# A graph attention kernel: the carried row taken from column 0 of the one-hots, superchunks of up to 112 nodes, and a longer memset between gathers

## The chip, the cores and the metric

The kernel runs on one core of one Trainium2 chip. The metric is the device time of one execution in microseconds. Times of "before" are a median of three runs; durations of single instructions come from one execution that the hardware profiler recorded.

## The reference

A graph of N = 6250 nodes with D = 256 features and E = 200000 edges, sorted by destination. Each edge has 32 attributes. After a layer norm and a relu of x, two graph attention layers follow: the first has 4 heads of 64 features, the second one head of 256. Each node also has an edge to itself.

```python
def _gat(x, src, dst, ea, Wg, a_s, a_d, Wge, a_e, b, n, h, f):
    hx = (x @ Wg).reshape(n, h, f)
    he = (ea @ Wge).reshape(-1, h, f)
    al = jax.nn.leaky_relu(jnp.einsum('nhf,hf->nh', hx, a_s)[src] + jnp.einsum('nhf,hf->nh', hx, a_d)[dst] + jnp.einsum('ehf,hf->eh', he, a_e), 0.2)
    m = jax.ops.segment_max(al, dst, num_segments=n)
    al = jnp.exp(al - m[dst])
    al = al / jax.ops.segment_sum(al, dst, num_segments=n)[dst]
    out = jax.ops.segment_sum(hx[src] * al[:, :, None], dst, num_segments=n)
    return out.reshape(n, h * f) + b
...
te = jax.nn.relu(edge_attr @ We0 + be0) * jnp.exp(x @ Wo0 + bo0)[src][:, None]
s2, d2, ea2 = _add_self_loops(src, dst, te, n)
x = jax.nn.relu(_gat(x, s2, d2, ea2, Wg0, as0, ad0, Wge0, ae0, bg0, n, HEADS, PH) + x)
```

The heavy part is that a row of the table of node features is fetched for every edge, scaled by the edge's weight, and summed over the edges of each destination.

## The kernel before

Edges are cut into chunks of P = 128, one edge in each partition, and C = 24 chunks make a superchunk, a "step". Each layer has 66 steps (the last two have 14 and 13 chunks), 132 in all. Since edges are sorted, the edges of a step belong to a run of some hundred consecutive nodes; `base` is the first of them, and `loc` says which of the run each edge belongs to.

In a step k, POOL fetches the source rows: `gather` (line 918) issues an indirect DMA per chunk (line 928) into the tile G, 24 of them, and behind each a memset of a small tile `gap` (line 932), which nothing reads. G has three buffers, so the gather of step k + 3 may start when the sums of step k have been made, and POOL runs ahead of the other engines. VectorE (DVE) adds up the logits of the edges (`logits`, line 1115 onward), finds maxima by segment with scans, and multiplies G by the edges' weights (`scale`, line 1223). `onehots` (line 1051) compares `loc` with a row of the numbers 0 to 127, `k_iota`, which stands in PSUM: S has for each edge a 1 in the column of its node. `sums` (line 1227) multiplies S by G on TensorE (PE), 24 matmuls, which the profile records as 48: the tile u in PSUM holds in row j the sum of node `base` + j. ScalarE (ACT) copies u to the tile U in SBUF (`evict`, line 1236); U has three buffers. `finish`, `rows1`, `rows2` and `rows3` divide by the sum of weights, add the self loop and the bias, make the node's row of the next layer's table T1 (layer 0) or of the output (layer 1), and store it.

A node whose edges begin in one step and end in the next needs the partial sum of the first step. `carry` (line 1241) selects that row of U, the row of the step's last node, by a matmul with the column `lsel` (line 1245, one-hot of the last node) into the PSUM tile `fin`, and ACT copies it into the tile `carry` (line 1247). `carried` (line 1197, on DVE) scales it and adds it to the first edge's row of the next step's G before that step's sums.

The order of the work is written out by hand in `edges` (main loop, lines 644 to 707): for step k and its successor nx, `gather(nx)`, the logits of k, edge features of nx on PE and ACT (`rphase1`, `rphase2`), the maxima and scale of k, `carried`, `sums`, then `edge_rows` and `onehots` of nx, `finish` of the step before, `evict`, `carry`, `rows1`. The last steps of a layer go through `tight` (line 727) and `last` (line 789), in which the sums are made in pieces and `carry` stands in other places. `nodes` (line 989) loads the rows of T and x of a step's nodes into the tile tw with SP's queue, 128 rows each, from a row that `base_i` gives; tw has five buffers.

Every engine works off its own queue in order. A wait of an instruction holds all that stands behind it on its engine.

Of the kernel before, what the change touches and what calls it, by code (L numbers as in the profile page):

```python
# [36 lines left out]
ED = 32  # L37
PH = 64
BIG = 1e38
PAD_DST = 1 << 20  # L40
END_DST = 1 << 22
EPS = 1e-5
# [36 lines left out]
class Kernel:  # L79
# [31 lines left out]
    def consts(self, wp):  # L111
# [33 lines left out]
                       allow_small_or_imprecise_dtypes=True)  # L145

        self.kps = k = self.ps_k.tile([P, 512], F32, name="kps")
        V.tensor_copy(k[:, 0:P], self.iota_f)
        m32 = wp.tile([P, 1], F32, name="m32", bufs=1)
        self.quad = cp.tile([P, 4], F32, name="quad")  # L150
        nc.gpsimd.memset(self.quad, 0.0)
# [2 lines left out]
            nc.gpsimd.memset(m32[r, :], -32.0 * i)  # L154
            nc.gpsimd.memset(self.quad[r, i:i + 1], 1.0)
        V.tensor_add(k[:, P:P + 1], self.iota_p, m32)
        self.k_iota, self.k_part, self.k_w = k[:, 0:P], k[:, P:P + 1], k[:, 2 * P:2 * P + 4 * C + 4]
        self.wea = []
        for L in self.L:
            wea = cp.tile([P, PH], F32, name=f"wea{L.l}")  # L160
# [236 lines left out]
    def fixed_rows(self):  # L397
        nc, cp = self.nc, self.cp
        self.crow = cp.tile([1, D + self.L[0].H], F32, name="crow")
        self.cl = [cp.tile([36, P + 1], F32, name=f"cl{i}") for i in range(2)]  # L400
        for t in self.cl:
            nc.gpsimd.memset(t, -BIG)

        self.cnt = cp.tile([P, self.NS, 2], F32, name="cnt")
        self.mt = cp.tile([P, 4 * C + 4], F32, name="mt")
        self.gap = cp.tile([P, 128], F32, name="gap")
        self.fb = [cp.tile([P, 37 * C], F32, name=f"fb{i}") for i in range(2)]
        for t in [self.mt] + self.fb:
            nc.gpsimd.memset(t, 0.0)


        self.aq = [cp.tile([P, 4, 32], BF, name=f"aq{i}") for i in range(2)]
        for t in self.aq:
            nc.gpsimd.memset(t, 0.0)
        self.trow1 = []
        L1 = self.L[1]
        for i in range(2):
            self.trow1.append(cp.tile([P, 2 * L1.TW], F32, name=f"t1row{i}"))
            nc.gpsimd.memset(self.trow1[i][:, L1.TW + D:], 0.0)
# [10 lines left out]
    def indices(self, wp):  # L430
# [26 lines left out]
        V.tensor_sub(qd, base.unsqueeze(1).to_broadcast([P, 4, NS]), qbase)  # L457
        yield
        self.qsel = cp.tile([P, NS, 4], F32, name="qsel")
        V.tensor_scalar(self.qsel.rearrange("p s k -> p k s"), qd, self.iota_p, None, op0=OP.add)  # L460
        yield

        bcf = wp.tile([NS, 4], F32, name="bcf", bufs=1)
# [29 lines left out]
        yield  # L493
        self.base_i = cp.tile([1, 2, NS], I32, name="base_i")
        V.tensor_copy(self.base_i[:, 0, :], base[0:1, :])
        V.tensor_scalar(self.base_i[:, 1, :], base[0:1, :], float(N - P), None, op0=OP.min)
        yield
        ll = wp.tile([P, NS], F32, name="ll", bufs=1)
        V.tensor_sub(ll, last, base)
        self.lsel = cp.tile([P, NS], F32, name="lsel")  # L500
        V.tensor_scalar(self.lsel, ll, self.iota_p, None, op0=OP.is_equal)
        yield
        self.slink = cp.tile([1, NS], F32, name="slink")
        V.tensor_tensor(self.slink, sc0[0:1, 0, :], sc0[0:1, 2, :], op=OP.is_equal)
# [2 lines left out]

        chk = wp.tile([1, 9, NS + 1], F32, name="chk", bufs=1)
        V.memset(chk, 0.0)
        V.tensor_scalar(chk[:, 0, :NS], ll[0:1, :], float(P - 1), None, op0=OP.is_gt)  # L510
        V.tensor_sub(qd[0:1], qlast[0:1], qbase[0:1])
        V.tensor_scalar(chk[:, 5:9, :NS], qd[0:1], 31.0, None, op0=OP.is_gt)
        nb = wp.tile([1, NS + 1], F32, name="nb", bufs=1)
# [1 line left out]
        yield  # L515
        V.memset(nb[:, NS:], float(N))
        V.tensor_sub(nb[:, :NS], nb[:, 1:], nb[:, :NS])
        V.tensor_scalar(chk[:, 1, :NS], nb[:, :NS], float(P), None, op0=OP.is_gt)
        V.tensor_scalar(chk[:, 2, :NS], nb[:, :NS], 0.0, None, op0=OP.is_lt)
        yield  # L520
        V.tensor_tensor(chk[:, 3, :NS], sc0[0:1, 0, :], sc0[0:1, 2, :], op=OP.is_lt)
        if self.direct:
            V.tensor_scalar(chk[:, 4, :self.direct], base[0:1, :self.direct], float(N - P), None, op0=OP.is_gt)
        V.memset(self.bad[:, 0:1], 0.0)
        V.tensor_reduce(self.bad[0:1, 0:1], chk.rearrange("p a b -> p (a b)"), axis=AX.X, op=OP.add)
        yield
# [84 lines left out]
    def edges(self, ctx):  # L611
# [11 lines left out]
        steps = self.steps  # L623
        self.state = {0: None, 1: None}
        self.early = 0
        self.nodes(steps[0])
        self.gather(steps[0], self.CX)
        if self.NS % 2:
# [15 lines left out]
        for k, st in enumerate(steps):  # L644
            nx = steps[k + 1] if k + 1 < len(steps) else None
            for q in steps[k + 1:k + 3]:
                if q["L"] is st["L"] and "tw" not in q:
                    self.nodes(q)
            self.load_lb(k + 2)
            left = self.groups[self.ahead][0] - 2 - k if self.ahead < len(self.groups) else 99  # L650
            if self.rest is None and left <= 2:
                gi = self.index_load(self.ahead, self.xp)
                self.rest = self.index_group(self.ahead, self.xp, gi)
            if st["s"] + 1 == self.NS:
                self.last(st, pv, nx)
# [24 lines left out]
            self.adst(nx)  # L680
            if "S" not in st:
                self.onehots(st)
            drain(self.scale(st))
            self.carried(st)
            if enter:
                self.begin(st, nx)
            else:
                self.sums(st)
            if late:
                self.rows3(late)  # L690
                late = None
            self.edge_rows(nx)
            self.onehots(nx)
            if pv:
                drain(self.finish(pv))
            if enter:
                pr = pv
            else:
                self.evict(st)
                self.carry(st)  # L700
                if pv:
                    self.rows1(pv)
                    late = pv
            self.index_on(left)
            pv = st
            if k == 0 and self.early:
                self.redirect()
# [19 lines left out]
    def tight(self, st, pv, pr, nx):  # L727
# [36 lines left out]
            self.rows3(pv)  # L764
        drain(self.maxima(st))
        if final:
            self.carry(pv)
            drain(y)
            self.load_ea(st["k"] + 2)
        else:  # L770
# [1 line left out]
        self.rphase2(nx)  # L772
        self.adst(nx)
        if not final:
            self.carry(pv)
            if pr:
                self.rows1(pr)
                self.rows2(pr)
# [10 lines left out]
    def last(self, st, pv, nx):  # L789
# [20 lines left out]
        drain(self.maxima(st))  # L810
        if pv:
            self.evict(pv)
            self.carry(pv)
        drain(self.scale(st, 3))
        self.carried(st)
        self.sums(st)
# [167 lines left out]
    def row(self, i, s):  # L984

        return self.nc.values_load(self.base_i[0:1, i, s:s + 1], engines=(mybir.EngineType.SP,), min_val=0,
                                   max_val=self.N - i * P, skip_runtime_bounds_check_because="destinations are nodes")

    def nodes(self, st):
        nc, L, s = self.nc, st["L"], st["s"]  # L990
        r = self.row(0, s)
        tw = self.np_.tile([P, self.L[0].TW + D], F32, name="tw", bufs=5)
        st["tw"], st["xw"] = tw[:, :L.TW], tw[:, L.TW:L.TW + D]
        w = L.TW + L.l * D
        nc.sync.dma_start(tw[:, :w], self.T[L.l][ds(r, P), 0:w])
        if L.l == 0:
            nc.sync.dma_start(st["xw"], self.a["x"][ds(r, P), :])

    def halves(self, st):

# [30 lines left out]
    def spread(self, st):  # L1031
# [6 lines left out]
        if len(q) < 2 or q[0]["C"] != q[1]["C"]:  # L1038
# [3 lines left out]
        Q = self.wp.tile([P, 2, P], BF, name="Q")  # L1042
        V.tensor_tensor(lb[:, :, :n], lb[:, :, :n], self.k_part.unsqueeze(2).to_broadcast([P, i, n]), op=OP.is_equal)  # L1043
        V.tensor_tensor(Q[:, :i].rearrange("p i (k j) -> p (i k) j", j=32),
                        self.k_iota[:, 0:32].unsqueeze(1).to_broadcast([P, 4 * i, 32]),
                        self.qsel[:, s:s + i, :].rearrange("p i k -> p (i k)").unsqueeze(2)
                        .to_broadcast([P, 4 * i, 32]), op=OP.is_equal)
        for j, t in enumerate(q):
# [2 lines left out]
    def onehots(self, st, c0=0, c1=C):  # L1051
        nc, o = self.nc, st["o"]
        c1 = min(c1, st["C"])
        if "S" not in st:
            st["S"] = self.sp.tile([P, C, P], F32, name="S")
        if c0 < c1:
            w = [P, c1 - c0, P]
            nc.vector.tensor_tensor(st["S"][:, c0:c1, :], self.k_iota.unsqueeze(1).to_broadcast(w),  # L1058
# [138 lines left out]
    def carried(self, st):  # L1197


        if st["prev"] is not None:  # L1200
            L, V = st["L"], self.nc.vector
            H, pr = L.H, st["pr"]
            g, cv = st["G"][0:1, 0, :], st["prev"]["carry"]
            if H == 1:
                V.scalar_tensor_tensor(g[:, :D + 1], cv[0:1, :D + 1], pr[:, 0:1], g[:, :D + 1], op0=OP.mult, op1=OP.add)
            else:
# [29 lines left out]
    def evict(self, st):  # L1236
        L = st["L"]
        st["U"] = U = self.np_.tile([P, 272], F32, name="U", bufs=3)
        self.nc.scalar.activation(U[:, :L.W], st["u"][:, :L.W], AF.Copy)  # L1239

    def carry(self, st):
        nc, L, s, U = self.nc, st["L"], st["s"], st["U"]
        if s + 1 < self.NS:
            pr = self.ps_f.tile([P, 512], F32, name="fin")
            nc.tensor.matmul(pr[0:1, :L.W], self.lsel[:, s:s + 1], U[:, :L.W], start=True, stop=True)  # L1245
            st["carry"] = cv = self.wp.tile([1, 272], F32, name="carry")
            nc.scalar.activation(cv[:, :L.W], pr[0:1, :L.W], AF.Copy)

    def merge(self, st, wp, w):

# [114 lines left out]
    def rows3(self, st):  # L1365
        nc, L, s = self.nc, st["L"], st["s"]
        if L.l == 0:
            self.table_row(st)
            r = self.row(0, s)
            nc.sync.dma_start(self.T[1][ds(r, P), :], st["trow"])  # L1370
            return
        o, out = st["o"], self.a["out"]
        if s < self.direct:
            r = self.row(1, s)
            nc.sync.dma_start(out[ds(r, P), :], o)
        else:
            idx = self.np_.tile([P, 1], I32, name="oidx")
            nc.vector.tensor_add(idx, self.base_f[:, s:s + 1], self.iota_p)
            nc.gpsimd.indirect_dma_start(
                out=out[:, :], out_offset=bass.IndirectOffsetOnAxis(ap=idx[:, 0:1], axis=0), in_=o,  # L1380
                in_offset=None, bounds_check=self.N - 1, oob_is_err=False)
# [215 lines left out]
```

## Time and profile before

| | |
|---|---|
| median of three runs | 4719.46 us (4714.36 to 4720.51) |
| profiled execution | 4718.23 us |
| its span, first to last instruction | 4716.0 us |
| mean granted TensorE clock | 0.732 |
| PE, DVE, ACT, POOL busy | 68%, 61%, 12%, 78% of the span |
| gathers (L928) | 3102, 959 ns each |
| memsets of `gap` (L932) | 3102, 221 ns each |
| carry matmul (L1245) | 260 records, busy 132.8 us in all |
| data moved | 584.09 MB, mean 124 GB/s |

A row of the groups reads: line, engine, operation, tile written and tiles read, how often, then busy time in all and ns of one, then the engine's idle time just ahead of them and what ended it. A row of the waits reads: who waited, for what, the sum of the time in us, how often, and the longest one. A row of the timeline reads: start in us, duration in us, engine, line, operation, how often (consecutive ones are merged), and in brackets the idle time ahead of it and its releaser. "remote" is a releaser that the profile can't place. A row of the windows reads: the stretch and its length, then for PE, PE's weight loads, DVE, ACT and POOL the busy time and the number of instructions, then the granted clock, the DMA engines' share, and GB/s.

### The profile page before, as it was taken

Reading aid. Unit: us, or ns where it says so; the run is one execution under the profiler, and the core shown is the slowest. Engines: PE = TensorE matmul, PEld = TensorE weight load, DVE = VectorE, ACT = ScalarE, POOL = GpSimd, SP = SyncE. Lnnn points to the kernel's source line nnn. Section 1 sums busy time; section 2 is a strip of 40 time slices with the busy share of each in tenths; the row PEclk is TensorE's granted clock in tenths of the full one; section 3 lists DMA queues with packets and bytes.
Section 4 is the critical chain, followed back from the end, with each engine's and each line's share of the span. In section 5 each row is a group of like instructions: output and inputs, shape, how many; then the busy total and the mean of one; then the engine's idle time right before and its main releaser. Section 6 shows DMA issues by size and latency. Waiting matters only on the chain.

```text
span 4716.0 us, 38255 instructions
## 1 busy us (share of the span) xinstructions
PE 3214.2 (68%) x10176; PEld 1915.8 (41%) x10176; DVE 2878.5 (61%) x6552; ACT 574.2 (12%) x1282; POOL 3701.8 (78%) x6350
## 2 busy tenths in 40 slices
PE   7777767777677776777655666666666666656666
PEld 6444444444444443444422333434333343433334
DVE  7566767667676676766743555546455555645555
ACT  5111111111111111111100001000000100000010
POOL 5688888888888888888648888888888888888884
PEclk9677777767777777777866677777767776777778
DMA  6344444444444444444323444444444444444442
GB/s 216 111 129 126 136 122 129 134 122 135 127 134 127 124 136 123 132 131 124 107 84 104 128 118 126 125 112 127 120 127 118 126 126 111 127 118 128 118 124 63
DMA packets 236364, 584.09 MB, mean 124 GB/s; under 512 B 63097, under 2 KB 91007, under 8 KB 236073
## 3 DMA queue, kind: packets, MB, share of 16 engines
q0 software_dynamic: 150144, 422.75, 33.8%
q1 hardware_dynamic: 85579, 158.16, 10.1%
q8 instruction: 82, 1.34, 0.1%
q14 instruction: 143, 1.17, 0.1%
q10 hardware_dynamic: 416, 0.67, 0.1%
HBM read 547.11 MB, written 34.33 MB: 123 GB/s over the span
## 4 chain that ended last, share of the span: by engine, by line
DVE 40%; another core or an unknown queue 33%; PE 16%; issue 6%; ACT 4%; POOL 0%; DMA 0%; SPq 0%; DVEq 0%; ACTq 0%; POOLq 0%
DVE G L1223 16%; DVE S L1058 8%; PE y L1014 8%; PE fin L1245 3%; DVE rt L1101 2%; ACT R L1019 1%; ACT U L1239 1%; DVE ade L1104 1%; PE fin L1329 1%; PE u L1234 1%; PE lf L1138 1%; PE zad L1028 1%; DVE mt L1172 1%; DVE m L1175 1%
## 5 line engine op out<-in xcount | busy, mean ns | idle before, releaser
L928 POOL DMA_INDIRECT G<-T,src x3102 | 2974.0, 959 | 938.3 <-issue 498.2
L1234 PE MATMUL u<-G,S 128*128 128x270 f32 (+1 forms) x6252 | 1469.7, 393 | 110.3 <-issue 58.0
L1234 PEld LDWEIGHTS u<-G,S 128*128 128x128 f32 x6252 | 1186.9, 192 | 394.5 <-issue 87.1
L1245 PE MATMUL fin<-U,lsel 128*1 128x270 f32 (+1 forms) x260 | 132.8, 613 | 1143.3 <-ACT U L1239 1136.6
L1223 DVE TENSOR_TENSOR G<-G,kps 128x6144 f32<-128x6144 f32 (+2 forms) x140 | 853.3, 6100 | 0.0
L1014 PE MATMUL y<-ea,webd 64*128 64x384 f32 (+1 forms) x1056 | 754.6, 866 | 89.2 <-issue 65.5
L932 POOL MEMSET gap<- 128x128 f32 x3102 | 684.6, 221 | 4.3 <-remote 1.3
L1148 DVE TENSOR_TENSOR_SCAN cl<-fl,cl,lf 4x129 f32<-4x129 f32 (+1 forms) x130 | 61.2, 471 | 1016.6 <-PE zad L1073 994.3
L1245 PEld LDWEIGHTS fin<-U,lsel 128*1 128x1 f32 x260 | 11.1, 81 | 1202.6 <-ACT U L1239 1201.5
L1028 PE MATMUL zad<-R,wea 128*64 128x384 f32 (+1 forms) x1056 | 474.0, 816 | 0.3 <-DVE aq L1080 0.3
L1014 PEld LDWEIGHTS y<-ea,webd 64*128 64x128 f32 x1056 | 303.3, 317 | 360.3 <-issue 330.0
L1058 DVE TENSOR_TENSOR S<-kps,loc 128x3072 f32<-128x3072 f32 x132 | 436.2, 3305 | 0.0
L1019 ACT ACTIVATE R<-y,webd 128x768 f32<-128x768 f32 x260 | 232.9, 896 | 794.6 <-PE y L1014 348.3
L1028 PEld LDWEIGHTS zad<-R,wea 128*64 128x64 f32 x1056 | 160.4, 207 | 314.9 <-issue 248.5
L1239 ACT ACTIVATE U<-u 128x270 f32<-128x270 f32 (+1 forms) x132 | 51.8, 393 | 1627.1 <-remote 1585.4
L1101 DVE STREAM_TRANSPOSE rt<-zad 128x768 f32<-128x768 f32 (+1 forms) x130 | 125.0, 961 | 27.8 <-remote 15.7
L424 PE MATMUL fin<-wg,h1T 128*128 128x260 f32 x264 | 135.7, 669 | 3.2 <-ACT h1T L1331 3.2
L1043 DVE TENSOR_TENSOR lb<-lb,kps 128x1536 bf16<-128x1536 bf16 (+1 forms) x68 | 113.0, 1662 | 0.0
L424 PE MATMUL ps<-wg,hT 128*128 128x266 f32 x292 | 89.8, 435 | 25.4 <-ACT hT L311 13.9
L424 PEld LDWEIGHTS fin<-wg,h1T 128*128 128x128 f32 x264 | 76.0, 317 | 53.7 <-issue 36.3
L1272 ACT ACTIVATE mw<-mw,mg 128x2 f32<-128x2 f32 x66 | 19.7, 298 | 557.3 <-DVE mw L1264 249.1
L1138 PE MATMUL lf<-ident,fb 128*36 128x128 f32 (+1 forms) x132 | 54.9, 416 | 42.8 <-DVE al L1119 28.2
(193 smaller groups left out, 2269.0 us busy)
## 6 DMA issues: line engine op xcount, KB each, us to landing
G<-T,src POOLq DMA_INDIRECT x3102
ea<-in_ea_dram SPq DMA_DIRECT2D x64, 768.0 KB
lb<-locrow SPq DMA_DIRECT2D x64, 384.0 KB
T<-t1row SPq DMA_DIRECT2D x66, 260.0 KB
tw<-T SPq DMA_DIRECT2D x66, 258.0 KB
tw<-T SPq DMA_DIRECT2D x66, 134.0 KB
tw<-in_x_dram SPq DMA_DIRECT2D x66, 128.0 KB
out_dram<-fb SPq DMA_DIRECT2D x64, 128.0 KB
```

Of the source, the lines that this page charges most:

```text
L424: self.nc.tensor.matmul(ps[:, :L.MW], hT[:, k, :], self.wg[L.l][:, k, :], start=(k == 0), stop=(k == 1))
L928: nc.gpsimd.indirect_dma_start(out=G[:, c, 0:L.TW], out_offset=None, in_=self.rows[L.l][0:n * (1 + L.l), :], in_offset=bass.IndirectOffset ...
L932: nc.gpsimd.memset(self.gap, 0.0)
L1014: nc.tensor.matmul(y[:, o], self.webd[l][r, :], ea[r, w], start=True, stop=True)
L1019: nc.scalar.activation(R[:, i, :32 * c].rearrange("p (b n) -> p b n", b=2), y.rearrange("p (b n) -> p b n", b=2)[:, :, :16 * c], AF.Relu, ...
L1028: nc.tensor.matmul(st["zad"][i * PH:(i + 1) * PH, o], self.wea[l][0], R[:, i, w], start=True, stop=False)
L1043: V.tensor_tensor(lb[:, :, :n], lb[:, :, :n], self.k_part.unsqueeze(2).to_broadcast([P, i, n]), op=OP.is_equal)
L1058: nc.vector.tensor_tensor(st["S"][:, c0:c1, :], self.k_iota.unsqueeze(1).to_broadcast(w), self.loc[:, o + c0:o + c1].unsqueeze(2).to_broad ...
L1101: V.transpose(rv[:, :32 * c].rearrange("p (b n) -> p b n", b=2), z.rearrange("p (b n) -> p b n", b=2)[:, :, :16 * c])
L1223: nc.vector.tensor_tensor(v, v, pw[:, c0:c1, :].unsqueeze(3) .to_broadcast([P, c1 - c0, H, L.F]), op=OP.mult)
L1234: nc.tensor.matmul(st["u"][:, :L.W], S[:, i, :], G[:, i, 0:L.W], start=(j == 0), stop=(j == c - 1))
L1245: nc.tensor.matmul(pr[0:1, :L.W], self.lsel[:, s:s + 1], U[:, :L.W], start=True, stop=True)
```

## The change

There are three parts.

1. Column 0 of S becomes a one-hot of the step's last node, and node j stands in column j + 1. Before the one-hots of a step, DVE copies a column of 128 elements, `lastloc` of that step, over column 0 of `k_iota`. Row 0 of u and U is then the row to carry. The function `carry` goes, with its matmul and its copy, and `carried` reads row 0 of the previous step's U.
2. A step may span up to M = 112 nodes instead of 128. The loads of tw and x, the stores of T1 and of the output cover 112 rows, in partitions 1 to 112. tw becomes five fixed tiles that DVE sets to zero once; a copy of the numbers 0 to 31 (`k_32`) and an index that starts at −1 (`iota_m`) are kept beside the old ones.
3. The tile `gap` has 208 elements in each partition instead of 128, so each memset covers 208.

```diff
+M = 112
...
-        V.tensor_copy(k[:, 0:P], self.iota_f)
+        V.tensor_scalar(k[:, 0:P], self.iota_f, -1.0, None, op0=OP.add)
+        V.tensor_copy(k[:, P + 2:P + 34], self.iota_f[:, 0:32])
...
-        self.gap = cp.tile([P, 128], F32, name="gap")
+        self.gap = cp.tile([P, 208], F32, name="gap")
...
-        ll = wp.tile([P, NS], F32, name="ll", bufs=1)
+        self.lastloc = ll = cp.tile([P, NS], F32, name="lastloc")
         V.tensor_sub(ll, last, base)
-        self.lsel = cp.tile([P, NS], F32, name="lsel")
-        V.tensor_scalar(self.lsel, ll, self.iota_p, None, op0=OP.is_equal)
...
+        self.tws = [self.np_.tile([P, self.L[0].TW + D], F32, name=f"tw{i}", bufs=1) for i in range(5)]
+        for t in self.tws:
+            nc.vector.memset(t, 0.0)
...
                 self.evict(st)
-                self.carry(st)
...
-        tw = self.np_.tile([P, self.L[0].TW + D], F32, name="tw", bufs=5)
+        tw = self.tws[st["k"] % 5]
...
-        nc.sync.dma_start(tw[:, :w], self.T[L.l][ds(r, P), 0:w])
+        nc.sync.dma_start(tw[1:M + 1, :w], self.T[L.l][ds(r, M), 0:w])
...
             st["S"] = self.sp.tile([P, C, P], F32, name="S")
+            nc.vector.tensor_copy(self.k_iota[:, 0:1], self.lastloc[:, st["s"]:st["s"] + 1])
...
-            g, cv = st["G"][0:1, 0, :], st["prev"]["carry"]
+            g, cv = st["G"][0:1, 0, :], st["prev"]["U"]
...
-    def carry(self, st):
-        nc, L, s, U = self.nc, st["L"], st["s"], st["U"]
-        if s + 1 < self.NS:
-            pr = self.ps_f.tile([P, 512], F32, name="fin")
-            nc.tensor.matmul(pr[0:1, :L.W], self.lsel[:, s:s + 1], U[:, :L.W], start=True, stop=True)
-            st["carry"] = cv = self.wp.tile([1, 272], F32, name="carry")
-            nc.scalar.activation(cv[:, :L.W], pr[0:1, :L.W], AF.Copy)
...
-            nc.sync.dma_start(self.T[1][ds(r, P), :], st["trow"])
+            nc.sync.dma_start(self.T[1][ds(r, M), :], st["trow"][1:M + 1, :])
...
-            nc.sync.dma_start(out[ds(r, P), :], o)
+            nc.sync.dma_start(out[ds(r, M), :], o[1:M + 1, :])
```

`carry` is called at four places, in the main loop, twice in `tight` and once in `last`; all four calls go.

More of the change, by code (lines that the diff above doesn't have):

```diff
@@ L147, in consts @@
         self.kps = k = self.ps_k.tile([P, 512], F32, name="kps")
-        V.tensor_copy(k[:, 0:P], self.iota_f)
+        V.tensor_scalar(k[:, 0:P], self.iota_f, -1.0, None, op0=OP.add)
+        V.tensor_copy(k[:, P + 2:P + 34], self.iota_f[:, 0:32])
+        self.iota_m = cp.tile([P, 1], F32, name="iota_m")
+        nc.gpsimd.iota(self.iota_m, pattern=[[0, 1]], base=-1, channel_multiplier=1,
+                       allow_small_or_imprecise_dtypes=True)
         m32 = wp.tile([P, 1], F32, name="m32", bufs=1)
@@ L156, in consts @@
         V.tensor_add(k[:, P:P + 1], self.iota_p, m32)
-        self.k_iota, self.k_part, self.k_w = k[:, 0:P], k[:, P:P + 1], k[:, 2 * P:2 * P + 4 * C + 4]
+        self.k_iota, self.k_part, self.k_32 = k[:, 0:P], k[:, P:P + 1], k[:, P + 2:P + 34]
+        self.k_w = k[:, 2 * P:2 * P + 4 * C + 4]
         self.wea = []
@@ L459, in indices @@
         self.qsel = cp.tile([P, NS, 4], F32, name="qsel")
-        V.tensor_scalar(self.qsel.rearrange("p s k -> p k s"), qd, self.iota_p, None, op0=OP.add)
+        V.tensor_scalar(self.qsel.rearrange("p s k -> p k s"), qd, self.iota_m, None, op0=OP.add)
         yield
@@ L495, in indices @@
         V.tensor_copy(self.base_i[:, 0, :], base[0:1, :])
-        V.tensor_scalar(self.base_i[:, 1, :], base[0:1, :], float(N - P), None, op0=OP.min)
+        V.tensor_scalar(self.base_i[:, 1, :], base[0:1, :], float(N - M), None, op0=OP.min)
         yield
-        ll = wp.tile([P, NS], F32, name="ll", bufs=1)
+        self.lastloc = ll = cp.tile([P, NS], F32, name="lastloc")
         V.tensor_sub(ll, last, base)
-        self.lsel = cp.tile([P, NS], F32, name="lsel")
-        V.tensor_scalar(self.lsel, ll, self.iota_p, None, op0=OP.is_equal)
         yield
@@ L509, in indices @@
         V.memset(chk, 0.0)
-        V.tensor_scalar(chk[:, 0, :NS], ll[0:1, :], float(P - 1), None, op0=OP.is_gt)
+        V.tensor_scalar(chk[:, 0, :NS], ll[0:1, :], float(M - 1), None, op0=OP.is_gt)
         V.tensor_sub(qd[0:1], qlast[0:1], qbase[0:1])
@@ L517, in indices @@
         V.tensor_sub(nb[:, :NS], nb[:, 1:], nb[:, :NS])
-        V.tensor_scalar(chk[:, 1, :NS], nb[:, :NS], float(P), None, op0=OP.is_gt)
+        V.tensor_scalar(chk[:, 1, :NS], nb[:, :NS], float(M), None, op0=OP.is_gt)
         V.tensor_scalar(chk[:, 2, :NS], nb[:, :NS], 0.0, None, op0=OP.is_lt)
@@ L522, in indices @@
         if self.direct:
-            V.tensor_scalar(chk[:, 4, :self.direct], base[0:1, :self.direct], float(N - P), None, op0=OP.is_gt)
+            V.tensor_scalar(chk[:, 4, :self.direct], base[0:1, :self.direct], float(N - M), None, op0=OP.is_gt)
         V.memset(self.bad[:, 0:1], 0.0)
@@ L766, in tight @@
         if final:
-            self.carry(pv)
             drain(y)
@@ L774, in tight @@
         if not final:
-            self.carry(pv)
             if pr:
@@ L812, in last @@
             self.evict(pv)
-            self.carry(pv)
         drain(self.scale(st, 3))
@@ L986, in row @@
         return self.nc.values_load(self.base_i[0:1, i, s:s + 1], engines=(mybir.EngineType.SP,), min_val=0,
-                                   max_val=self.N - i * P, skip_runtime_bounds_check_because="destinations are nodes")
+                                   max_val=self.N - i * M, skip_runtime_bounds_check_because="destinations are nodes")
     def nodes(self, st):
@@ L991, in nodes @@
         r = self.row(0, s)
-        tw = self.np_.tile([P, self.L[0].TW + D], F32, name="tw", bufs=5)
+        tw = self.tws[st["k"] % 5]
         st["tw"], st["xw"] = tw[:, :L.TW], tw[:, L.TW:L.TW + D]
         w = L.TW + L.l * D
-        nc.sync.dma_start(tw[:, :w], self.T[L.l][ds(r, P), 0:w])
+        nc.sync.dma_start(tw[1:M + 1, :w], self.T[L.l][ds(r, M), 0:w])
         if L.l == 0:
-            nc.sync.dma_start(st["xw"], self.a["x"][ds(r, P), :])
+            nc.sync.dma_start(st["xw"][1:M + 1, :], self.a["x"][ds(r, M), :])
     def halves(self, st):
@@ L1044, in spread @@
         V.tensor_tensor(Q[:, :i].rearrange("p i (k j) -> p (i k) j", j=32),
-                        self.k_iota[:, 0:32].unsqueeze(1).to_broadcast([P, 4 * i, 32]),
+                        self.k_32.unsqueeze(1).to_broadcast([P, 4 * i, 32]),
                         self.qsel[:, s:s + i, :].rearrange("p i k -> p (i k)").unsqueeze(2)
@@ L1374, in rows3 @@
             r = self.row(1, s)
-            nc.sync.dma_start(out[ds(r, P), :], o)
+            nc.sync.dma_start(out[ds(r, M), :], o[1:M + 1, :])
         else:
             idx = self.np_.tile([P, 1], I32, name="oidx")
-            nc.vector.tensor_add(idx, self.base_f[:, s:s + 1], self.iota_p)
+            nc.vector.tensor_add(idx, self.base_f[:, s:s + 1], self.iota_m)
+            nc.vector.memset(idx[0:1, :], 1 << 20)
             nc.gpsimd.indirect_dma_start(
```

## The prediction

> **What bounds the kernel now.** I read the busy shares first, then the costliest groups, then the waits, then one step of layer 0 in the timeline, and last the windows over that step for the granted clock.
>
> ```profile
> PE 3214.2 (68%) x10176; PEld 1915.8 (41%) x10176; DVE 2878.5 (61%) x6552; ACT 574.2 (12%) x1282; POOL 3701.8 (78%) x6350
> ...
> L928 POOL DMA_INDIRECT G<-T,src x3102 | 2974.0, 959 | 938.3 <-issue 498.2
> ...
> L932 POOL MEMSET gap<- 128x128 f32 x3102 | 684.6, 221 | 4.3 <-remote 1.3
> ```
>
> No engine is full. POOL is nearest: of its 3701.8 us, 3658.6 are the 3102 gathers and the memset behind each. One gather with its memset takes 959 + 221 ns and two gaps of some 0.16 us in all, so POOL starts one every 1.337 us. 24 of them are 32.1 us, but the steps (from one eviction U to the next, 60 regular ones in each layer) last 34.60 us in layer 0 and 34.43 in layer 1. POOL waits for something once a step.
>
> ```profile
> ACT U L1239 <- remote: 1585.4, 123, 58.5
> PE fin L1245 <- ACT U L1239: 1136.6, 123, 18.2
> POOL G L928 <- remote: 285.9, 120, 3.0
> ```
>
> In 120 steps POOL stands about 2.4 us, and ACT before U far longer, for a signal that the profile can't place. The timeline of one step tells what it is:
>
> ```profile
> 1499.74 0.95 POOL L928 DMA_INDIRECT G<-T,src  x1 [2.39 <-remote]
> ...
> 1515.10 11.27 PE L1234 MATMUL u<-G,S 128*128 128x270 f32 x48 [0.33 <-issue]
> ...
> 1530.60 0.95 POOL L928 DMA_INDIRECT G<-T,src  x1 [0.17 <-DVE a L1068]
> ...
> 1534.25 0.40 ACT L1239 ACTIVATE U<-u 128x270 f32<-128x270 f32 x1 [9.75 <-remote]
> 1534.49 0.95 POOL L928 DMA_INDIRECT G<-T,src  x1 [2.71 <-remote]
> 1534.70 1.06 PE L1245 MATMUL fin<-U,lsel 128*1 128x270 f32 x2 [8.34 <-ACT U L1239]
> 1535.79 0.39 ACT L1247 ACTIVATE carry<-fin 1x270 f32<-1x270 f32 x1 [1.15 <-PE fin L1245]
> 1536.23 0.69 PE L1329 MATMUL fin<-ident,fb 128*128 128x128 f32 x2 [0.48 <-ACT carry L1247]
> ```
>
> PE's last record of the sums u ends at 1526.4, and U, which needs nothing but u, starts at 1534.25. In the first step, where no gather is in flight during u, the same 48 records take 11.35 us and U follows in 0.02 us. So either PE still works, or its signal is late. The windows decide: the granted clock is 1.00 until 1527, 0.98 in 1527 to 1529, and 0.50 from there on.
>
> ```profile
> 1525.00:1527.00 2.00, 1.36 (x6) 0.78 (x5) 0.56 (x3) 0.00 (x0) 1.67 (x4) 1.00 0.48 146
> 1527.00:1529.00 2.00, 0.00 (x0) 0.00 (x0) 0.50 (x2) 0.00 (x0) 1.83 (x4) 0.98 0.49 139
> 1529.00:1531.00 2.00, 0.00 (x0) 0.00 (x0) 0.82 (x3) 0.00 (x0) 1.67 (x4) 0.50 0.32 82
> ```
>
> From 1527 PE has no record (0.00, x0), and its clock falls to the 0.50 that it also shows before u; were it still at work on u at full clock, the clock would hold. So PE is done, the signal is late, and it is late as long as gathers stream. U comes at a fixed distance from the batch's first gather (34.4 us in layer 0, 34.2 in layer 1), hardly moved by when u began. One batch of layer 1 began 1.5 us late with u on time (first gather 4140.32), and U was 1.5 us late too (4174.45). The batches of 13 give 18.6 us, that of 72 gathers 102.0. From these three, U stands at about 0.25 + 1.413 n us behind the first of n gathers, while POOL issues every 1.337. While signals are late DVE's small dependent operations are late as well, by 0.4 to 1.1 us each; in steps where POOL had one more pause of 0.28 us few of them are. I read this as a path that signals share with POOL's gathers: POOL at 1.337 fills it, and what is over waits. So a step is POOL's batch plus a late signal, not PE's or DVE's work. From U to the next u is 15.4 us (layer 0) or 13.3 (layer 1); with 11.35 for u that makes 26.8 and 24.6, which would be the step if no gather held it.
>
> By **the Trainium skill, SBUF — State Buffer, section Who interferes with whom**, only the port pair of VectorE and GpSimd contends, and DMA with no engine. The first step's 11.35 us against 19.1 to U here doesn't contradict it, since PE is idle, not slowed, but then nothing in SBUF explains the late signal, and a wait for the gathers' landing is what is left. By that rule the time would be the first rival's below, 4782, and by my reading of the rows 4640.
>
> **The change, part by part.**
>
> *The longer memset.* No row has 208 elements. POOL memsets of 128, 536 and 888 elements take 221, 552 and 848 ns, 0.81 to 0.84 ns an element. So 80 elements more are 65 ns, the memset 286 ns, the pitch 1.402 us, and a batch of 24 takes 33.65. The batches now run 0.2 us over 24 pitches through POOL's waits for other events; I keep that: 33.85. POOL's busy time rises by 3102 × 0.065 = 202 us. Now 1.402 is nearly the 1.413 at which the path moves in the long run. What is left over per gather falls from 0.076 to 0.011 us. After a batch's end the whole of the late signals is through within 0.7 us (last landing about 33.4, U at 34.1), so 48 records cost about 0.015 us or less each; 0.065 us more per gather are room for four, and the 13 gathers that run beside u make room for about 50. So I expect U early enough that POOL doesn't wait for it, and the step to be POOL's batch alone: 33.85 us. Layer 0 gains 60 × 0.75 = 45 us, layer 1 60 × 0.58 = 35 us. Together −80.
>
> *The carry.* Two PE records and an ACT copy go from 128 steps. Between U and the next PE operation (L1329) that is 1534.25 to 1536.23: 1.98 us of layer 0's chain, 1.4 us in layer 1. This is on PE's chain, but that chain (26.8 and 24.6) lies under POOL's 33.85, so it gives 0. If the chain did bound the step, 34.60 − 1.98 = 32.6 would lie under POOL's 33.85 too: the answer is the same. Reading U's row 0 instead adds no wait, as U was already older than the carry. In the last three steps of each layer, where POOL has less to do, part of it may count: 3 us taken, between 0 and 10.
>
> *Column 0 and the copy.* One DVE copy of 128x1 a step. No such row; a 32x1 POOL memset takes 91 ns, a 128x2 ACT operation 298. 132 × 0.09 to 0.30 = 12 to 40 us of DVE, beside 994 us that DVE waits for PE at L1148. I take 0; if DVE were late, the upper end is 40.
>
> *112 rows.* The five transfers of a step (258, 134, 128, 260, 128 KB) lose an eighth, some 7.4 MB of 584. At 124 GB/s it would be 59 us if transfers ended the steps; SP's queue fills 10.1% of the engines and no long wait names tw, so 0. Five DVE memsets of 128x526 at the start are 5 × 0.55 (the 128x536 row of POOL): +3 us ahead of layer 0.
>
> The sum: 4716.0 − 80 − 3 + 3 = 4636, with 2.2 around the span 4638. The profiled execution (4718.2) lies 1.2 under the median, so 4640. With U in time but POOL's pitch held at the long batch's late 1.415, the step is 34.16 and the time 4676; with none of the 0.2 us it is 4615. **Own range 4612 to 4680.**
>
> **Rivals.** *U is tied to the landing of the batch's last gather* (slower). For it: every regular U follows that landing by 0 to 0.7 us, the batches of 13 too, where no backlog can have grown (last gather 4670.13, U 4672.67, 2.54 later), and POOL's other pauses never let U out before. Against it: U needs no gather of that batch, and the distance from last gather to U isn't fixed (2.54 of 13, 3.3 of 24, 4.06 of 72), nor does a longer batch move U by its whole length. Its price: the last gather starts at 23 × 1.402 = 32.25; with 2.54 to U and 0.25 to the restart, the step is 35.04, +0.44 and +0.61, together +63: 4782. With today's 3.3, +1.2 and +1.37: +154, 4873. It decides if U still comes behind the last landing, since POOL then pays its 1.5 us each step and the carry's 2 us are under cover.
>
> *Nothing moves* (same). The path serves a gather in 1.413 whatever POOL does, and 0.011 us a gather still keep it full: U stays at 34.2 to 34.4, POOL only waits 1.5 us less. 4715 to 4725.
>
> *The change doesn't do what it says:* the memset is absorbed in the 0.16 us of gaps beside it, pitch 1.337. Then again 4719. Its row is busy time and the gaps are the same behind every gather, so this has little, and goes with the former.
>
> **Chances.** POOL alone bounds: 0.50. Tied to the landing: 0.36. Nothing moves: 0.14. The range reaches from the first case's low end into the second, to 4800; left out are the upper part of the tied case (about 0.17) and a little below. About 0.2% (9 us) is what a measurement of this kernel can tell from no change: faster 0.50, same 0.14, slower 0.36.
>
> **What would show it.** The gap row at 286 ns and the pitch at 1.40 (the memset). L1245 and L1247 gone, and PE's L1329 or L1138 straight behind U (the carry). POOL's wait for "remote" (285.9 us) gone, ACT's (1585.4) far smaller, and U ahead of the batch's last gather: my case. If instead U stands 2.5 to 3.3 us behind the last gather and POOL's remote wait is kept, the landing decides. If U stays at 34.2 to 34.4 from the first gather with POOL's wait near 1 us, nothing moves. I would be wrong throughout if some wait of DVE's for PE, now 994 us, ended last in each step.

## The result and the profile after

The changed kernel took 4707.74 us (median of 12 runs, 4702.77 to 4727.87) against 4717.36 for the kernel before (12 runs): ratio of the means 0.9984, 95% interval 0.9976 to 0.9991. I had forecast 4640, a gain of 1.7%; what came is a tenth of that and within the 0.2% that I called no change. The wide range, 4612 to 4800, holds it by luck, since it reaches over the rivals; the range of my own case, 4612 to 4680, does not.

One thing has to be known for what follows: in this and two other groups of runs the kernel before took 4717 to 4754 us, and in three others 4378, one chip having stood on both sides, so that every ratio below is against the kernel before of its own group, and the groups are called slow-signal and prompt. In two of the prompt groups one execution of the kernel before took over 5200 us; these two are left out of the ratios.

The costliest groups of the changed kernel, POOL's two rows:

```profile
L931 POOL DMA_INDIRECT G<-T,src x3102 | 2972.6, 958 | 723.2 <-issue 519.4
...
L935 POOL MEMSET gap<- 128x208 f32 x3102 | 893.2, 288 | 1.5
```

The memset is 288 ns, 286 were forecast, and the pitch, the time from the start of one gather to that of the next, is 1.403 us, 1.402 forecast. POOL's idle time before gathers fell from 938.3 to 723.2 us. In the waits view the releasers of those waits are scattered:

```profile
ACT U L1243 <- remote: 1239.0, 78, 38.5
...
POOL G L931 <- remote: 43.6, 30, 2.2
POOL G L931 <- PE zad L1077: 36.6, 12, 6.0
POOL G L931 <- PE u L1238: 23.6, 4, 8.5
```

POOL's 285.9 us for "remote" are 43.6, but with the two rows of PE beside it they make some 104, and ACT still waits 1239 us before U, which is late. Two steps of layer 0 in the timeline, one after the other, show both ways it can go:

```profile
1374.11 11.29 PE L1238 MATMUL u<-G,S 128*128 128x270 f32 x48 [0.33 <-DVE G L1217]
...
1389.02 0.40 ACT L1243 ACTIVATE U<-u 128x270 f32<-128x270 f32 x1 [5.20 <-PE y L1017]
...
1403.26 11.21 PE L1238 MATMUL u<-G,S 128*128 128x270 f32 x48 [2.06 <-issue]
...
1430.48 0.40 ACT L1243 ACTIVATE U<-u 128x270 f32<-128x270 f32 x1 [17.56 <-remote]
1430.71 0.95 POOL L931 DMA_INDIRECT G<-T,src  x1 [1.25 <-remote]
```

In the first, u ends at 1385.4 and U starts at 1389.0 while POOL goes on gathering. In the second, u ends at 1414.5 and U starts 16 us later, 0.2 us before POOL's next gather: POOL had stopped, since it lacked a free G buffer, and only then the signal came. Counted over the regular steps, POOL paused (over 1.95 us from one gather to the next) 118 times before and 41 times after; U came with POOL at a stop in 117 of 118 steps before, in 40 of 118 after. In the chain that ended last, POOL has taken DVE's place; the first line is of before, the second of after:

```profile
DVE 40%; another core or an unknown queue 33%; PE 16%; issue 6%; ACT 4%; POOL 0%; DMA 0%; SPq 0%; DVEq 0%; ACTq 0%; POOLq 0%
...
POOL 45%; DVE 17%; issue 15%; PE 15%; another core or an unknown queue 7%; ACT 1%; DMA 1%; DVEq 0%; POOLq 0%; SPq 0%; ACTq 0%
```

The regular steps, from the first gather of one to that of the next, are 34.60 us in layer 0 (34.60 before) and 34.55 in layer 1 (34.42 before): nothing gained. What POOL's 41 pauses last beyond one pitch is 84 us, as much as the forecast gain. The 9 us come from the ends of the layers. The last U of layer 0 lies at 2395.4 (2402.4 before); from the first gather of layer 1's step 62 (counted from 0) to the last U it takes 137.9 us (148.1 before).

### The profile page after: what moved, and what is told of

Its sections match the earlier page's. It is cut to its first block, busy times and chain, and to the rows that moved or that the text cites. A ratio compares the mean times of both kernels' runs of the same rounds, so it can differ in the third digit from the quotient of the medians.

```text
span 4706.9 us, 37631 instructions
## 1 busy us (share of the span) xinstructions
PE 3159.1 (67%) x9916; PEld 1890.3 (40%) x9916; DVE 2909.7 (62%) x6691; ACT 518.0 (11%) x1152; POOL 3908.9 (83%) x6351
## 4 chain that ended last, share of the span: by engine, by line
POOL 45%; DVE 17%; issue 15%; PE 15%; another core or an unknown queue 7%; ACT 1%; DMA 1%; DVEq 0%; POOLq 0%; SPq 0%; ACTq 0%
POOL G L931 34%; POOL gap L935 10%; PE u L1238 7%; DVE G L1227 5%; PE y L1017 3%; DVE S L1062 2%; PE zad L1031 1%; PE ps L430 1%; PE fin L430 1%; DMA G<-T,src 1%; DVE lb L1046 1%; DVE rt L1105 1%; DVE mt L1176 0%; DVE m L1179 0%
## 5 line engine op out<-in xcount | busy, mean ns | idle before, releaser
L931 POOL DMA_INDIRECT G<-T,src x3102 | 2972.6, 958 | 723.2 <-issue 519.4
L1238 PE MATMUL u<-G,S 128*128 128x270 f32 (+1 forms) x6252 | 1618.1, 411 | 381.7 <-issue 289.5
L1238 PEld LDWEIGHTS u<-G,S 128*128 128x128 f32 x6252 | 1236.5, 200 | 753.9 <-issue 393.7
L935 POOL MEMSET gap<- 128x208 f32 x3102 | 893.2, 288 | 1.5
L1017 PE MATMUL y<-ea,webd 64*128 64x384 f32 (+1 forms) x1056 | 659.2, 759 | 206.8 <-issue 155.6
L1031 PE MATMUL zad<-R,wea 128*64 128x384 f32 (+1 forms) x1056 | 489.9, 809 | 44.7 <-issue 27.8
L1159 PE MATMUL lf<-ident,cl 36*128 36x36 f32 (+1 forms) x132 | 38.2, 289 | 617.1 <-DVE cl L1154 341.1
L1017 PEld LDWEIGHTS y<-ea,webd 64*128 64x128 f32 x1056 | 262.6, 273 | 430.3 <-issue 338.9
L1159 PEld LDWEIGHTS lf<-ident,cl 36*128 36x128 f32 (+1 forms) x132 | 23.5, 178 | 706.6 <-DVE cl L1154 383.2
L1142 PE MATMUL lf<-ident,fb 128*36 128x128 f32 (+1 forms) x132 | 41.8, 317 | 125.1 <-DVE al L1125 52.2
L1077 PE MATMUL zad<-a,Q 128*128 128x12 bf16 (+1 forms) x132 | 23.6, 179 | 96.8 <-DVE a L1075 36.3
```

Source lines behind the costliest of these rows:

```text
L931: nc.gpsimd.indirect_dma_start(out=G[:, c, 0:L.TW], out_offset=None, in_=self.rows[L.l][0:n * (1 + L.l), :], in_offset=bass.IndirectOffset ...
L935: nc.gpsimd.memset(self.gap, 0.0)
L1017: nc.tensor.matmul(y[:, o], self.webd[l][r, :], ea[r, w], start=True, stop=True)
L1031: nc.tensor.matmul(st["zad"][i * PH:(i + 1) * PH, o], self.wea[l][0], R[:, i, w], start=True, stop=False)
L1159: nc.tensor.transpose(pc, cl[:n, 0:P], self.ident[0:n, 0:n])
L1238: nc.tensor.matmul(st["u"][:, :L.W], S[:, i, :], G[:, i, 0:L.W], start=(j == 0), stop=(j == c - 1))
```

## The experiments

**Theory A**: signals are held while gathers stream, the carry lies under cover, and the longer memset lets some signals through at the price of its own time. **Theory B**: the carry was the gain and the memset a loss. The first four kernels change the memset alone, on one chip, with the kernel before at 4754.39 us.

```diff
-        self.gap = cp.tile([P, 208], F32, name="gap")
+        self.gap = cp.tile([P, 128], F32, name="gap")
```

> The changed kernel with the gap memset back at 128 elements: column 0 and the 112 rows alone. Theory A (signals are held while gathers stream and pass when POOL drains, so the carry lies under cover): POOL waits for U in every step again, steps of 34.4 to 34.6 us, time 4708 to 4717, no more than 0.2% below the kernel before. Theory B (the carry on PE's chain was the gain, and the longer memset costs): steps shorter by 0.3 us or more, time below 4690.

Ratio 1.0000 (0.9991 to 1.0008). POOL stops at U 118 times again. Column 0 and the 112 rows together, without the longer memset, are worth nothing there, as A has it.

The kernel before with 208 elements:

> The kernel before with the gap memset at 208 elements, nothing else. Theory A: the same mixture as in the changed kernel (POOL waits for U in some 40 of 120 steps instead of 120, pitch 1.403), time 4700 to 4720. Theory B: the longer memset is a loss by itself, 4730 to 4780.

Ratio 1.0017 (1.0007 to 1.0028), 4760.77 us, 82 pauses. The memset alone is a small loss, between what A and B expected (both worked out beside 4717 us). So neither part gains alone. The changed kernel's 0.9984, with both, is of another group of runs.

> The changed kernel with a gap of 288 elements: the memset about 352 ns, the pitch 1.468. Theory A, if what passes grows with the room between two gathers: POOL never waits, the step is 24 x 1.468 + 0.2 = 35.4 us, +0.8 on 120 steps, 4810. If U is tied to the landing of the last gather all the same: 23 x 1.468 + 3.3 + 0.25 = 37.3 us, 5040.

Ratio 1.0066 (1.0051 to 1.008), 4783.43 us. Steps are 35.42 and 35.40 us, 35.4 expected; the wait for "remote" is gone from POOL and from ACT. The waits view has no more than this of ACT before U:

```profile
ACT U L1243 <- PE u L1238: 343.5, 74, 19.1
ACT U L1243 <- issue: 170.4, 58, 5.3
```

and the chain is POOL's:

```profile
POOL 83%; issue 11%; PE 3%; DVE 2%; ACT 0%; DMA 0%; ACTq 0%; another core or an unknown queue 0%; POOLq 0%; DVEq 0%
```

In the median step U now starts 0.04 us after u's last matmul; with 128 elements on the same chip it was 12 us (layer 0) and 14 us (layer 1). This is the state that I had forecast for 208 elements.

> The changed kernel with a gap of 16 elements: the memset about 90 to 130 ns, the pitch about 1.22. If the step is POOL's batch plus a fixed wait for the drain (23 x pitch + 3.3 + 0.25): 31.6 us, -3 us on 120 steps, 4350. If the path serves a gather in 1.41 us whatever POOL does: steps of 34.2 to 34.5 and 4700 to 4720, with POOL's own gathers or its wait longer by what the memset gives up.

Ratio 1.0346 (1.0331 to 1.0361): issuing faster made it slower. Both expectations failed. The pitch is 1.26 us. In the median step U follows u's last matmul in 0.04 us, but u itself is stretched, to 22 us (layer 0) and 24 us (layer 1) in place of 11; one u in the timeline:

```profile
1523.98 7.86 PE L1238 MATMUL u<-G,S 128*128 128x270 f32 x33 [0.33 <-issue]
1533.07 0.39 PE L1238 MATMUL u<-G,S 128*128 128x270 f32 x1 [1.23 <-issue]
1536.56 0.61 PE L1238 MATMUL u<-G,S 128*128 128x270 f32 x1 [3.10 <-issue]
1538.67 0.61 PE L1238 MATMUL u<-G,S 128*128 128x270 f32 x1 [1.50 <-issue]
1541.45 4.45 PE L1238 MATMUL u<-G,S 128*128 128x270 f32 x12 [2.18 <-issue]
```

33 records run, then PE takes one every two to three and a half us until POOL has stopped (its last gather begins at 1536.4), and the last 12 run without a wait. What is held is not only the last signal but PE's own progress. Which part of the chip holds it, no run shows.

The next four ran on another chip, the kernel before at 4746.12 us.

> The changed kernel with a gap of 224 elements, pitch about 1.416 us. Theory A2 (a threshold: while POOL starts gathers faster than one per about 1.41 us, signals are held until it drains; above it they pass and POOL never waits for U): the step is 24 x 1.416 + 0.2 = 34.2 us, 0.4 us under the changed kernel's 34.6, ratio to before about 0.989. Theory B2 (no threshold, the room between gathers only lets a share of the signals through): some 20 waits are left of the 44 with 208 elements, steps of 34.5, ratio 0.997 to 1.000.

Ratio 0.9959 (0.9945 to 0.9972), 34 pauses: neither the threshold of A2 nor quite B2. The pauses are those of the slowest of its six executions (4749 us, the median is 4729).

> The changed kernel with a gap of 240 elements, pitch about 1.430 us. A2: POOL never waits for U, 24 x 1.430 + 0.2 = 34.5 us, ratio 0.997. B2: 10 waits are left, 34.7 us, ratio 1.002.

Ratio 0.9935 (0.9922 to 0.9949): **faster than the kernel before**, and a lower ratio than the changed kernel had in its own group (0.9984); the changed kernel itself did not run in this one. 13 pauses are left, but U is still 10 to 12 us late:

```profile
ACT U L1243 <- remote: 1431.3, 99, 20.7
```

It is late, but before POOL needs it. So there are two points: the pitch at which POOL no longer meets a late U (mostly, at 1.430), and that at which U is no longer late (between 1.430 and 1.468, by runs on two chips).

> The changed kernel with one part undone: the carried row goes through a PE matmul with the first column of the identity and an ACT copy again, before the same work as in the kernel before. If the carry costs nothing beside POOL's pace: ratio as the changed kernel's, 0.998. If it is the part that separates the changed kernel (0.9984) from the kernel before with 208 elements (1.0017): ratio 1.001 to 1.002.

```diff
+    def carry(self, st):
...
+            nc.tensor.matmul(pr[0:1, :L.W], self.ident[:, 0:1], U[:, :L.W], start=True, stop=True)
+            st["carry"] = cv = self.wp.tile([1, 272], F32, name="carry")
+            nc.scalar.activation(cv[:, :L.W], pr[0:1, :L.W], AF.Copy)
...
-            g, cv = st["G"][0:1, 0, :], st["prev"]["U"]
+            g, cv = st["G"][0:1, 0, :], st["prev"]["carry"]
```

Ratio 1.0027 (1.0016 to 1.0038), 80 pauses, where the kernel before with 208 had 82. This points to column 0, not the 112 rows, as what separates the changed kernel from that one by some 0.4%; but the three ratios come from three groups, so it is not shown. The carry copy starts 1.5 us after U whether POOL streams or not, so its hops are not held. That 1.5 to 2 us more from U to the next u bring the next U that much closer to POOL's stop is my reading, not shown.

> The changed kernel with a gap of 288 elements, where POOL never waits, and each matmul of the sums split in two by columns, so that PE issues twice the matmuls for the same sums. Theory A2 (the pace of the gathers alone decides): POOL still never waits for U, steps of 35.4 us, ratio 1.007. Rival (PE's own instructions fill the path together with the gathers): POOL waits for remote again, in most steps, steps over 36 us, ratio over 1.02.

```diff
-            nc.tensor.matmul(st["u"][:, :L.W], S[:, i, :], G[:, i, 0:L.W], start=(j == 0), stop=(j == c - 1))
+            for x, y in ((0, 128), (128, L.W)):
+                nc.tensor.matmul(st["u"][:, x:y], S[:, i, :], G[:, i, x:y], start=(j == 0 and x == 0), stop=(j == c - 1 and x > 0))
```

4783.23 us in one run, steps of 35.45 us, POOL without waits. But U is late again, by 5.7 us in layer 0 and 3.0 in layer 1, and the row that 288 elements had removed is back:

```profile
ACT U L1244 <- remote: 1049.7, 94, 21.2
```

Twice the matmuls for the same sums, at the same pace of gathers: this speaks for the rival that PE's own instructions take part in filling what the signals wait for, though POOL's waits did not come. It is one run, and the kernel without the split ran on the other chip, where signals were held no less (4754 us for the kernel before, 4746 here), so the group is an unlikely cause but not an excluded one.

In the next group the kernel before took 4378 us, and none of the four kernels had a late U.

> The kernel before with a gap of 240 elements, so without column 0 and the 112 rows. Theory C (the carry's two hops, ACT to PE and PE to ACT, are two more signals that come late once POOL no longer drains at U): ratio 0.998 to 1.003, at least 0.004 above the changed kernel with 240 elements (0.9935). If the pace alone makes the gain: 0.992 to 0.995.

Ratio 1.0608 (1.0593 to 1.0623), 4644.57 us, steps of 34.54 and 34.51. What I wanted to know of the carry was not tested, since nothing was late.

> The changed kernel with 128-element memsets and, behind the gather of the 16th chunk of a step, eight memsets of 208 in a row: POOL spends as long on a step as with 240 elements in each, but the room lies in one place (24 x 1.337 + 2.3 + 0.2 = 34.6 us). If the mean pace decides: ratio 0.993 to 1.000 and few waits of POOL for U. If the room must lie behind each gather (the path fills again within the eight gathers that follow): POOL waits for U in most steps, steps of 36 us or more, ratio over 1.03.

Ratio 1.0749, and 1.0751 and 1.0745 when it was run twice more; all three groups were prompt, where the question doesn't arise. Whether the room must lie behind each gather stays open.

> The changed kernel with 288 elements and two more loads of 112 rows of the table a step through SP's queue into a tile that nothing reads, some 12% more bytes. If the bytes that the DMA engines move take the room: U is late again by 3 us or more (it is 0.2 us late without them) and ACT's wait for remote comes back with some hundred us. If only POOL's gathers and PE's instructions count: U stays 0.2 us late, steps of 35.4 us.

4763.41 us, and U 0.04 us behind u's last matmul, but so it was in every kernel of the group. Open as well.

> The changed kernel with superchunks of up to 127 nodes, so that loads and stores cover 127 rows instead of 112. If the number of rows is nothing but bytes (13% more of the row transfers, no wait in the chain names them): ratio within 0.003 of the changed kernel's 0.998. If 127 rows, which 16 doesn't divide, are moved by fewer DMA engines: the loads of tw land several us later, SP's share falls on few engines, ratio over 1.01.

Ratio 1.0643 (1.0626 to 1.066), 4659.59 us, against 1.0432 for the changed kernel itself in another prompt group (below): 92 us more. The loss lies in layer 0, where a step has two such loads: its last U comes 83 us later, while the steps of layer 1 are 33.82 us against 33.86. A stretch of the chain that ended last, in layer 0, has what no other kernel showed: SP's issues of the loads of tw (L998) and x (L1000), and the load behind them.

```profile
1008.21 4.00 SPq L1366
1012.24 0.51 SPq L989
1012.95 9.39 SPq L998
1022.52 11.51 SPq L1000
1034.12 23.04 DMA lb<-locrow
1057.19 1.75 DVE lb L1046
```

The rows of the two lines, for 127 rows and then for 112 (the changed kernel in a prompt group), with the shortest, median and longest ns of an issue:

```profile
L998 SPq DMA_DIRECT2D tw<-T x132: 266/8150/19007, 118.6 to 4550.3; - x132
L1000 SPq DMA_DIRECT2D tw<-in_x_dram x66: 1064/11101/14232, 119.1 to 2310.3; - x66
```

```profile
L998 SPq DMA_DIRECT2D tw<-T x132: 317/328/1054, 118.5 to 4454.4; - x132
L1000 SPq DMA_DIRECT2D tw<-in_x_dram x66: 317/327/1082, 119.1 to 2220.2; - x66
```

8.15 us against 0.33. The Trainium skill, DMA: Bandwidth & Descriptors, section Why a DMA increments its semaphore by 16 and not by 1, says that a transfer is spread over the largest number of engines, up to 16, that divides its rows, and names 127 partitions as a case for one engine. The page gives no issue times, and the runs don't show the engines themselves, so fewer engines as the cause of the long issues is my reading. With column 0 taken, 128 rows no longer fit; 112 rows keep that from costing the 92 us that 127 cost here.

> The kernel before, unchanged, for its trace on the chip that this group runs on. Theory D (how fast gathers may follow each other before signals are held differs from chip to chip): where the kernel before takes about 4378 us, U starts within 0.3 us of u's last matmul, POOL never waits for U, and the step is 24 x 1.337 + 0.2 = 32.3 us; where it takes 4710 to 4755, U is 8 to 14 us late and the step is 34.4 to 34.9. Rival (the 4378 us come from something else, a faster clock or faster transfers): the same lateness of U in both, and other steps shorter.

4381.16 us, prompt. Steps of 32.39 and 32.42 us, U 0.04 us behind u's last matmul, POOL never at a stop for U: what theory D expects where the time is 4378.

```profile
1507.64 11.21 PE L1234 MATMUL u<-G,S 128*128 128x270 f32 x48 [0.33 <-DVE G L1213]
1518.89 0.40 ACT L1239 ACTIVATE U<-u 128x270 f32<-128x270 f32 x1 [1.92 <-PE u L1234]
```

The rival was faster transfers or a faster clock. The rows of POOL's DMA queue (packets, MB, the share of 16 engines' span that the packets took), in the slow-signal trace of before and then in this one, are

```profile
q0 software_dynamic: 150144, 422.75, 33.8%
...
q0 software_dynamic: 150144, 422.75, 36.3%
```

of 4716.0 and 4379.0 us, so 1594 and 1590 us: the transfers took as long in both. The 48 records of u took 11.21 us in the median step of layer 0 in both, too. What differs is when the signals come.

> The changed kernel, unchanged. D: on a chip where the kernel before takes about 4378 us POOL alone bounds both kernels, and the change costs 24 x 0.066 = 1.58 us in each of some 126 steps: 4570 to 4660, ratio 1.045 to 1.065. On a chip where it takes 4710 to 4755: ratio 0.997 to 1.001.

Ratio 1.0432 (1.0413 to 1.0451), 4567.42 us: **4.3% slower** here. Steps are 33.90 and 33.86 us, the 33.85 of my forecast, and the chain is POOL's:

```profile
POOL 83%; issue 12%; PE 3%; DVE 2%; DMA 0%; ACT 0%; POOLq 0%; ACTq 0%; DVEq 0%; SPq 0%
```

> The kernel before with a gap of 16 elements, pitch 1.26 us. D, on a chip where signals are held at 1.337: more is held, ratio 1.02 to 1.04. On a chip where they are not: either POOL alone still bounds, 24 x 1.26 + 0.2 = 30.4 us a step, ratio 0.945; or the point from which signals are held lies between 1.26 and 1.337 there, and U is late and the ratio over 0.97.

Ratio 0.9424 (0.9407 to 0.9441), 4126.18 us, steps of 30.42 and 30.33: POOL alone still bounds at a pitch of 1.26.

The changed kernel without the memset:

> The changed kernel without the memset behind each gather. On a chip where signals are not held at 1.26: POOL's pitch falls to some 1.05 us, 24 x 1.05 = 25.2 us, and the chain of PE and DVE (24.6 and 26.8 us in the trace of before) is next: steps of 25 to 28 us, 3450 to 3850, ratio 0.79 to 0.88; or U is late there too and the ratio is over 0.9. On a chip where they are held at 1.337: ratio over 1.03, as 1.035 with 16 elements.

Ratio 0.9385 (0.9369 to 0.94), 4109.28 us, **the fastest seen**, but only in a prompt group. I had guessed a pitch of 1.05; a gather's 954 ns are followed by 0.30 us without a memset too, so the pitch is 1.25, and steps are 30.31 and 30.10. This ran on the very chip on which the kernel before had taken 4746 us, and it took 4378 this time. So the late signals do not belong to a chip, as theory D had it, but to something that holds for a group of runs; what that is stays open.

## Why the prediction was wrong

**The memset and the pitch**: right to 2 ns, 1.403 for 1.402. **POOL's batch**: right; 24 pitches and 0.2 us are 33.85 us, and where nothing is late the changed kernel's steps are 33.90 and 33.86.

**The step that failed** is "So I expect U early enough that POOL doesn't wait for it, and the step to be POOL's batch alone". That term was 0; it measured 34.60 − 33.85 = 0.75 us a step in layer 0 and 0.70 in layer 1. POOL stopped 41 times, 84 us in all, and that took back all of the −80. The reasoning was short by its own figures: a pitch of 1.402 us is under a path's 1.413, so a backlog still grows by 0.011 us a gather, and slower growth is not free room. Two of the figures were wrong as well. The 1.413 us I took for the pace of the path came from how late U was, at one pitch; with 240 elements, pitch 1.430, U is still 10 us late, and only at 1.468 prompt. And the "room for four" signals in 0.065 us supposed a few records waiting for a gap; with 16 elements PE's own matmuls are held, and the split sums suggest that its whole stream of matmuls competes with the gathers, so that a little more room frees little. The mechanism was there: pauses fall 118, 41, 34, 13, 2 with 128, 208, 224, 240 and 288 elements, in three groups of runs, and one in each layer is left even where no U is late. Why signals are held at all stays open.

**The rival of the landing** had U tied to POOL's stop. That is how nearly each U of the kernel before and a third of those after came, but not the rest, and the time did not rise by 63. **Nothing moves** came nearest in time (4715 to 4725), for a wrong reason: POOL's wait did not merely shrink by what the memset took; it became rarer.

**The carry**: 0 was right with 128 elements (ratio 1.0000) and perhaps wrong at 208, where the kernel with the carry came out some 0.4% slower in another group. I had argued that PE's chain, 26.8 and 24.6 us, lies under POOL's batch; but U's lateness, 8 and 10 us before, belongs to that chain, and with it the chain is as long as the step. The ends of the layers, 3 us forecast, gave about 16; the regular steps of layer 1 lost the difference. The carry alone is not what gave them: with 128 elements, where it is gone too, layer 1's end takes 148.0 us, as before.

**The 112 rows**: 0 was right against 128, as far as column 0 and the rows together show (1.0000). **The starting memsets**: the five stand in the chain that ended last, from 140.29 to 143.02 us; 2.7 us for 3 forecast. **The copy per step** takes DVE 152 ns, 20 us in 132 steps; the chain has 2.1 us of it, so taking 0 was nearly right.

**What I could not see**: in the trace of before U was late in every step, and I took this for the kernel's nature. In a prompt group the change is a loss of 4.3%: the steps are 1.51 and 1.44 us longer, nearly the 24 × 0.066 = 1.58 us that the longer memset adds to a batch.

## What to carry to other kernels

Where a signal comes late although its sender has long been done, find what else runs in that time and vary its pace in both directions before costing an edit: here slower gathers lost their own time, gained it back in part, and faster ones (16 elements) lost 3.5% in the changed kernel in one group and won 5.8% in the kernel before in another. A pause put in to spare a busy path is worth only what the path's state makes it worth: time such a tuning in several sessions, and against the kernel without any pause. And look at how long the issue of a load takes when its number of rows changes: here 112 and 128 rows were cheap and 127 were not.

## What the runs showed of the hardware

- In the slow-signal groups a stream of indirect gathers held other engines' progress. With a gather every 1.337 us U started 7.7 us (layer 0) and 10.3 us (layer 1) after u's last matmul in the median step; with one every 1.26 us PE took one matmul record per two to three and a half us in the middle of u; with one every 1.468 us U followed in 0.04 us. In the prompt groups it did so even at 1.25 us. Twice the matmuls at 1.468 us, in one run on another chip, came with 3 to 6 us of lateness.
- The same program on the same chip took 4742 to 4750 us in one group of runs and 4374 to 4382 in another.
- An indirect DMA of 128 rows occupied POOL for 954 ns, and with nothing between two of them the second started 1.25 us after the first had started.
- A load of 127 rows held SP's queue 8.15 us at the median, one of 112 rows 0.33, and one of 128 rows 0.34.
